# A transformer block with experts on one core: weights loaded later, products spaced wider, and the rows of expert tiles fetched ahead of their weights

## The chip, the core and the metric

The kernel runs on one core of a Trainium2 chip. A core has five engines, each with its own queue of instructions, and they run side by side. PE (TensorE) multiplies matrices and transposes, DVE (VectorE) does elementwise work, reductions and scans, ACT (ScalarE) does activation functions and copies, POOL (GpSimd) does elementwise work and indirect transfers, and SP (SyncE) does no arithmetic here: it issues transfers between HBM and the core. The metric is the device time of one execution in microseconds (us).

## The reference, cut to what matters

Four images of 256 channels and 1024 positions go through one layer: a convolutional and attention part, and then a mixture of eight experts of which two are used for each position.

```python
def _L0_conv_ref(x, ...):                       # per image; C = 256, N = 1024
    xn = layernorm(xs, norm_w, norm_b)
    xm = mamba_v(xc, ...) + skip_scale * xc     # 4 groups of channels; a scan along the 1024 positions
    Q  = conv1d(conv1d(x_concat, qdw_w, groups=NB), qpw_w)
    xgt = sigmoid(Q) * xm
    R  = conv1d(conv1d(xgt, rdw_w, groups=C), rpw_w) + xgt        # depthwise of 3 taps, then a product
    xm2 = conv1d(conv1d(concat(xs, R), fdw_w, groups=2*C), fpw_w) + xs
    x_local  = conv1d(xm2, lc_w, groups=C)
    x_global = mha(xm2, ...)                    # 8 heads over 1024 positions
    x_out = gelu(layernorm(concat(x_local, x_global) @ fc_w.T + fc_b))
    xi = conv3x3_depthwise(ln_hw(x_out)) + dwc_b
    return layernorm(xi) @ proj_w.T + proj_b

x = x + _L0_conv_ref(_ln_c(x), ...)
def _L0_ffn_ref(x, Wg, bg, W1, b1, W2, b2):     # 4096 positions, 8 experts, top 2
    top_w, top_i = top_k(x @ Wg + bg, 2);  w = softmax(top_w)
    for e in range(8):
        out += w[:, e] * (gelu(x @ W1[e] + b1[e]) @ W2[e] + b2[e])
t = t + _L0_ffn_ref(_ln_t(t), ...)
```

## The kernel before, as far as the change touches it

The kernel writes its instructions in an order of its own. Each piece of work is a Python generator; a clock of **ticks** calls each generator when it is due, and `yield k` means "go on k ticks later". The order of the calls is the order of the instructions in each engine's queue, and nothing else is decided by a tick. The backbone is the scan of the mamba part: per image 8 parts of 16 steps, one step per tick (`dBu` and `hs` on DVE, `dA` on ACT, `bs` and `yp` on PE). Everything else of the earlier image is hung between these steps.

```python
def in_turn(items, make, use, lag=2, every=1):  # products on PE (make), and what takes them away (use)
    made, lag = [], lag // every
    for at in range(len(items) + lag):
        if at >= lag:
            use(items[at - lag], made[at - lag])
        if at < len(items):
            made.append(make(items[at]))
        yield every

def depthwise3(dst, c, src, c_src, w, wi, bias):   # one tap on ACT, two on DVE, a tick between them
    nc.scalar.activation(dst[:, c, :], src[:, c_src, 0:N], AF.Identity, ...)
    yield 1
    for k in (1, 2):
        nc.vector.scalar_tensor_tensor(dst[:, c, :], src[:, c_src, k : k + N], ...)
        yield 1

def later_weights():        # weights that only later stages need, on SP's queue
    ...                     # vb, qdwT, 4 x qpwT
    for t, ap in later:     # aoutT, projT, fcT, rpwT, fpwT, wvT
        nc.sync.dma_start(t, ap)
        yield 1
    ...                     # wqkT in two transfers, qk_b in four small ones, sums on PE and DVE

def convolutions(b):
    ...                     # d[0], d[1]: depthwise results; xm: the gated image
    def residual(at, r):    # xm += product (DVE)
        ...
    yield from in_turn(CO_H, lambda at: product(f"rp_{b}...", rpwT_s, at[0], [d[1]...]), residual)
    d[1] = a8(f"d4r_{b}")
    for c in range(NC2):
        yield from depthwise3(d[1], c, xm, c, "fdw_w", NC2 + c, ...)
    def mixed(at, r):       # xl += product (DVE)
        ...
    yield from in_turn(CO_H, lambda at: product(f"fp_{b}...", fpwT_s, at[0], [d[0], d[1]...]),
                       mixed, every=1 if b == B - 1 else 2)
    yield from prepared(b)  # v, q and k of the attention

def joined(b):              # after the attention
    ...
    yield from in_turn(CO_H, lambda at: product(f"fc_{b}...", fcT_s, ...),
                       lambda at, r: nc.scalar.activation(xc[...], r, AF.Identity, ...))
    ...

def around(b): ...          # norm over the image, 3x3 taps: 18 DVE instructions into xi
def sent_off(b):            # means and variances of xi (PE), projection, routing, rows scattered (POOL)
    ...
```

After the scans of the last image PE works through 35 tiles of the experts (256 rows each), and the tail of image 3 (convolutions, attention, joining, routing; counted from 0) and the third image's `around` and `sent_off` are hung between the steps of the tiles. The tiles of the second series (8 to 15) need the third image's rows, those from 16 on the last image's.

```python
def tiles():
    def load(n):            # table of experts and rows of a new series (DVE), then 2 MB of weights (SP)
        s, i = order[n]
        if i == 0:
            tables.append(experts.series(s, temp))
        ...
        got[n] = experts.load(s, i, tables[s], w1, w2, b2_s)
    def rows(n): ...        # 256 rows of XS (260 KB), SP
    def front(n): ...       # rows transposed: xp (PE), xT (DVE)
    def ahead(n, at):       # called at each step `at` of the tile before; one thing per call
        if n < len(order) and known(n) and n not in got:
            load(n)
        elif n in got and sent(n) and n not in xs and len(got[n]) == 4:
            rows(n)
        elif n in xs and at >= 5:
            front(n)
    for n in range(len(order)):
        ...
        for at, _ in enumerate(experts.tile(n, got[n], hs, ...)):   # 8 steps: 4 x h, 4 x y
            ahead(n + 1, at)
            yield T.get(("pace",), 1)                                # ticks between two steps

PACE = {"convolutions": 1.6, "product": 2, "norm": 1.2, "taps": 0.67, "routing": 1.3, "rows": 1}
```

The weights of two tiles fit: those of tile n + 1 go where those of tile n - 1 were. PSUM has eight buffers of 128 x 512, shared by all products and by `dBu`.

Of the kernel before, what the change touches and what calls it, by code (L numbers as in the profile page):

```python
# [72 lines left out]
def network(  # L73
# [45 lines left out]
    def col(name, i=0, rows=slice(0, P)):  # L119
        at = _AT[name] + i  # L120
        return V[rows, at : at + 1]
# [22 lines left out]
    with tc.tile_pool(name="w_conv", bufs=1) as wp, tc.tile_pool(  # L144
# [53 lines left out]
        def later_weights():  # L198

            nc.sync.dma_start(vb, vbias.rearrange("a (c p) -> p (a c)", p=P))  # L200
            for t in (qdwT_s, qpwT_s, qdw_b):
                nc.gpsimd.memset(t, 0.0)
            yield 1
            nc.sync.dma_start(
                qdwT_s[:, 0 : NC2 * 3 * NB], qdwT.rearrange("p c k n -> p (c k n)")
            )
            yield 1
            for i in range(4):
                nc.sync.dma_start(qpwT_s[32 * i : 32 * i + NB, :], qpwT)
                if i % 2 == 0:  # L210
                    at = _AT["qdw_b"]
                    nc.sync.dma_start(qdw_b[32 * i : 32 * i + NB, :], vecs[0:NB, at : at + 1])
                yield 1
            for t, ap in later:
                nc.sync.dma_start(t, ap)
                yield 1
            for ci in range(NC2):
                nc.sync.dma_start(
                    wqkT_s[:, ci].rearrange("p w (i x) -> p (w i) x", x=2 * HD)
                    .rearrange("p c (i x) -> p c i x", x=HD),  # L220
                    wqkT[:, ci].rearrange("p c (i x) -> p c i x", x=2 * HD)[:, :, :, 0:HD],
                )
                yield 1
            for i in range(4):
                at = _AT["qk_b"] + i // 2
                nc.sync.dma_start(
                    qk_b[ts(i, HD), :], vecs[ds(64 * (i % 2), HD), at : at + 8 : 2]
                )
                yield 1

            obp = ps_tile("obp")
            for co in range(NC2):
                for ci in range(NC2):
                    nc.tensor.matmul(
                        obp[:, co : co + 1], aoutT_s[:, ci, ts(co, P)], vb[:, ci : ci + 1],
                        start=(ci == 0), stop=(ci == NC2 - 1),
                    )
            yield 1
            nc.vector.tensor_tensor(
                ob, obp[:, 0:NC2], V[:, _AT["attn_outb"] : _AT["attn_outb"] + NC2], ALU.add  # L240
            )

            prp = ps_tile("prp")
            for co in range(NC2):
                for ci in range(NC2):
                    nc.tensor.matmul(
                        prp[:, co : co + 1], projT_s[:, ci, ts(co, P)], col("norm_b", ci),
                        start=(ci == 0), stop=(ci == NC2 - 1),
                    )
            yield 1  # L250
            nc.vector.tensor_tensor(
                prb, prp[:, 0:NC2], V[:, _AT["proj_b"] : _AT["proj_b"] + NC2], ALU.add
            )
            for ci in range(NC2):
                nc.vector.tensor_scalar(
                    projT_s[:, ci, :], projT_s[:, ci, :], col("norm_w", ci), None, ALU.mult
                )
            yield 1

            nc.vector.tensor_reduce(fcm, fcT_s, AX.X, ALU.add)  # L260
            yield 1
            nc.vector.tensor_scalar(fcm, fcm, 1.0 / C, None, ALU.mult)
            nc.vector.tensor_tensor(
                fcT_s, fcT_s, fcm.to_broadcast([P, 2 * NC2, C]), ALU.subtract
            )
            fbp = ps_tile("fbp")
            for c in range(NC2):
                nc.tensor.matmul(
                    fbp[:, 0:1], ones_mean, col("fc_b", c), start=(c == 0), stop=(c == NC2 - 1)
                )  # L270
            yield 1
            nc.vector.tensor_tensor(
                fcb, V[:, _AT["fc_b"] : _AT["fc_b"] + NC2], fbp[:, 0:1].to_broadcast([P, NC2]),
                ALU.subtract,
            )
# [67 lines left out]
        def a8(name):  # L343
            return act8.tile([P, NC2, N], F32, tag="a8", name=name)
# [13 lines left out]
        def half(h):  # L358
            return ts(h, HALF)
# [397 lines left out]
        def convolutions(b):  # L757
# [56 lines left out]
            def residual(at, r):  # L814
# [1 line left out]
                inner = xm[:, co, ds(1 + h * HALF, HALF)]  # L816
                nc.vector.scalar_tensor_tensor(inner, r, col("rpw_b", co), inner, ALU.add, ALU.add)

            yield from in_turn(
                CO_H, lambda at: product(  # L820
                    f"rp_{b}_{at[0]}_{at[1]}", rpwT_s, at[0],
                    [d[1][:, ci, half(at[1])] for ci in range(NC2)],
                ), residual,
            )
            d[1] = a8(f"d4r_{b}")
            for c in range(NC2):
                yield from depthwise3(d[1], c, xm, c, "fdw_w", NC2 + c, col("fdw_b", NC2 + c))

            def mixed(at, r):
                co, h = at  # L830
# [4 lines left out]
                CO_H, lambda at: product(  # L835
                    f"fp_{b}_{at[0]}_{at[1]}", fpwT_s, at[0],
                    [d[ci // 2][:, ci % 2, half(at[1])] for ci in range(4)],
                ), mixed, every=1 if b == B - 1 else 2,
            )
            yield from prepared(b)  # L840

# [205 lines left out]
        def joined(b):  # L1047

            xloc, oT = XLOC.pop(b), OT.pop(b)
            pace(b, PACE["product"])  # L1050
            xglo = a8(f"xglo_{b}")
            T["attending", b] = True
            yield from in_turn(
                CO_H, lambda at: product(
                    f"ao_{b}_{at[0]}_{at[1]}", aoutT_s, at[0],
                    [oT[ci][:, half(at[1])] for ci in range(NC2)],
                ),
                lambda at, r: nc.scalar.activation(
                    xglo[:, at[0], half(at[1])], r, AF.Identity, bias=ob[:, at[0] : at[0] + 1]
                ),  # L1060
            )

            xc = XC[b] = a8(f"xc_{b}")
            both = (xloc, xglo)
            yield from in_turn(
                CO_H, lambda at: product(
                    f"fc_{b}_{at[0]}_{at[1]}", fcT_s, at[0],
                    [both[ci // 2][:, ci % 2, half(at[1])] for ci in range(4)],
                ),
                lambda at, r: nc.scalar.activation(  # L1070
                    xc[:, at[0], half(at[1])], r, AF.Identity, bias=fcb[:, at[0] : at[0] + 1]
                ),
            )

            T["joining", b] = True
            pace(b, PACE["norm"])
            yield from inverse_deviation(f"lgn_{b}", xc, b == B - 1)
            for c in range(NC2):
                nc.scalar.activation(
                    xc[:, c, :], xc[:, c, :], AF.Gelu, bias=col("lgn_b", c), scale=col("lgn_w", c)  # L1080
                )
            loaded[0] = None
            log_exp()
            yield 2
# [44 lines left out]
        def sent_off(b):  # L1129

            xc = XC.pop(b)

            def centre(h, mean):
                for c in range(NC2):
# [39 lines left out]
        def tiles():  # L1174
# [15 lines left out]
            def sent(n):  # L1190
                return T.get(("sent", B - 3 + order[n][0]))

            def load(n):
                s, i = order[n]
                if i == 0:
                    tables.append(experts.series(s, temp))
                if n == 0:
                    w1 = [a8("w1_0")[:, :, 0:DFF]]
                    w2 = [a8("w2_0").rearrange("p c (k x) -> p (c k) x", x=C)]
                else:  # L1200
                    w = [
                        acts.tile([P, N], F32, tag="dts", name=f"w_{n}_{k}") for k in range(3)
                    ] + [actd.tile([P, N], F32, tag="dt", name=f"w_{n}_3")]
                    w1, w2 = w[0:2], [v.rearrange("p (k c) -> p k c", c=C) for v in w[2:4]]
                b2_s = actc.tile([P, C], F32, tag="cs", name=f"b2_{n}") if n else a2("b2_0")[:, 0:C]
                got[n] = experts.load(s, i, tables[s], w1, w2, b2_s)
# [12 lines left out]

            def ahead(n, at):  # L1220

                if n < len(order) and known(n) and n not in got:
                    load(n)
                elif n in got and sent(n) and n not in xs and len(got[n]) == 4:
                    rows(n)
                elif n in xs and at >= 5:
                    front(n)

            for n in range(len(order)):
                while n not in got or len(got[n]) == 4:  # L1230
# [63 lines left out]
        def whole(b):  # L1294
# [2 lines left out]
        PARTS = 2 * NB  # L1297

        PACE = {
            "convolutions": 1.6, "product": 2, "norm": 1.2, "taps": 0.67, "routing": 1.3, "rows": 1  # L1300
        }
        with tc.manual_schedule(engines=ALL):
            log_exp()
# [3 lines left out]
            for b in range(B):  # L1307
                for p in range(PARTS):
                    at = b * PARTS + p
                    stop = b > 0 and p == PARTS // 2 - 1 or at == len(parts) - 1  # L1310
                    if b == 0 and p == 0:
                        start(later_weights())
                    if b == 0 and p == 2:
                        start(normalised(1))
# [729 lines left out]
```

## Time and profile before

| what | value |
|---|---|
| time, median of 3 runs | 2439.6 us (2438.16 to 2451.21) |
| span of the profiled execution | 2441.0 us, 28282 instructions |
| PE busy | 2086.5 us (85%) |
| DVE busy | 1631.0 us (67%) |
| ACT busy | 1189.7 us (49%) |
| POOL busy | 1099.7 us (45%) |
| granted PE clock, mean | 0.911 |
| DVE scan, 512 instructions | 640.0 us, 1.22 to 1.28 us each |
| first and last scan | 60.1 us, 1634.3 us |
| a tile of the experts at full rate | 14.3 us from one to the next, PE alone |

The lines of the profile are read so: line of the kernel, engine, operation, result <- operands; a wait is named by what came last. The names that matter below: `fp` and `rp` are the products of the convolutions, `fc` that of the joining projection, `xl` and `xm` what they are added into, `xi` the image under the 3x3 taps, `xs` the rows of a tile, `w` its weights, `h` and `y` its two products.

### The profile page before, as it was taken

How to read it: one execution, taken by the hardware profiler on the slowest of the kernel's cores; microseconds unless marked ns; L12 is line 12 of the kernel's file. 1: busy time of each engine (PE TensorE's matmuls, PEld its weight loads, DVE VectorE, ACT ScalarE, POOL GpSimd, SP SyncE). 2: the span in 40 equal slices, each digit the busy share in tenths (PEclk: the TensorE clock that was granted, in tenths of full speed). 3: DMA queues.
4: the chain of work that ended last, by engine and by line, in shares of the span. 5: the costliest groups of instructions: out<-in, count | busy, mean ns of one | idle time of the engine just before them, and what ended most of it. 6: DMA issues, size and time to landing. Idle time of an engine off the chain costs nothing. (4 is left out here: it accounts for less than half of the span.)

```text
span 2441.0 us, 28282 instructions
## 1 busy us (share of the span) xinstructions
PE 2086.5 (85%) x8810; PEld 933.9 (38%) x8810; DVE 1631.0 (67%) x2255; ACT 1189.7 (49%) x2013; POOL 1099.7 (45%) x1185
## 2 busy tenths in 40 slices
PE   7778767899977699987769999667999988899995
PEld 2111111332311132222113323114733667788885
DVE  3888998875899988789988877986544253211111
ACT  4553555468654458764254776325267522122221
POOL 0677777631677760466776115571130114222221
PEclk7897998999998899998689999768999999999997
DMA  3534342220234230043332102342320357566665
GB/s 88 134 109 104 83 122 70 68 60 27 73 97 109 65 84 27 22 117 83 111 87 59 47 22 66 85 156 82 92 80 1 91 154 224 171 192 199 190 197 154
DMA packets 155021, 244.32 MB, mean 100 GB/s; under 512 B 34212, under 2 KB 103492, under 8 KB 154856
## 3 DMA queue, kind: packets, MB, share of 16 engines
q1 hardware_dynamic: 135680, 217.07, 31.1%
q0 software_dynamic: 13264, 17.85, 3.7%
q10 hardware_dynamic: 5912, 7.45, 0.9%
q8 instruction: 74, 1.21, 0.2%
q14 instruction: 91, 0.75, 0.1%
HBM read 141.17 MB, written 33.98 MB: 72 GB/s over the span
## 5 line engine op out<-in xcount | busy, mean ns | idle before, releaser
L623 POOL TENSOR_TENSOR hs<-hs,cs 128x512 f32<-128x512 f32 x512 | 672.8, 1315 | 214.1 <-DVE hs L618 158.2
L604 ACT ACTIVATE dA<-dts,A 128x512 f32<-128x512 f32 x512 | 343.0, 713 | 286.1 <-DMA dts<-dt 204.5
L629 PE MATMUL yp<-hs,quads 128*32 128x512 f32 x1024 | 344.7, 687 | 151.0 <-POOL hs L623 110.5
L611 DVE TENSOR_TENSOR dBu<-dts,bs 128x512 f32<-128x512 f32 x512 | 347.7, 679 | 50.7 <-ACT xc L1070 15.3
L1911 POOL DMA_INDIRECT Y<-ys,dest x70 | 110.9, 1585 | 561.4 <-DVE ys L1905 554.9
L618 DVE TENSOR_TENSOR_SCAN hs<-dA,last,dBu 128x512 f32<-128x512 f32 x256 | 327.6, 1280 | 25.2 <-ACT low L555 0.5
L618 DVE TENSOR_TENSOR_SCAN hs<-dA,dBu 128x512 f32<-128x512 f32 x256 | 312.4, 1220 | 38.3 <-ACT dA L604 13.7
L1890 ACT ACTIVATE hs<-h,b 128x256 f32<-128x256 f32 x280 | 117.0, 472 | 385.6 <-PE h L1885 198.2
L942 ACT ACTIVATE e<-st 128x512 f32<-128x512 f32 x512 | 262.5, 607 | 74.5 <-PE st L932 71.7
L1895 PE MATMUL y<-w,hs 128*128 128x256 f32 x1120 | 261.8, 386 | 5.9 <-ACT hs L1890 5.9
L1885 PE MATMUL h<-xT,w 128*128 128x256 f32 x1120 | 252.4, 381 | 1.6 <-DVE xT L1863 1.6
L1863 DVE COPY xT<-xp 128x512 f32<-128x512 f32 x35 | 24.2, 692 | 314.0 <-PE xp L1862 299.2
L622 POOL COPY last<-hs 128x1 f32<-128x1 f32 x256 | 70.8, 277 | 355.6 <-DVE hs L618 330.6
L1895 PEld LDWEIGHTS y<-w,hs 128*128 128x128 f32 x1120 | 214.2, 194 | 41.8 <-ACT hs L1890 7.2
L596 PE MATMUL bs<-u,xpwT_s 128*32 128x512 f32 x1024 | 184.5, 698 | 52.2 <-DVE hs L618 25.8
L1885 PEld LDWEIGHTS h<-xT,w 128*128 128x128 f32 x1120 | 213.0, 191 | 38.0 <-issue 7.3
L629 PEld LDWEIGHTS yp<-hs,quads 128*32 128x32 f32 x1024 | 56.6, 119 | 412.4 <-POOL hs L623 291.1
L984 DVE TENSOR_TENSOR e<-e,e 128x512 f32<-128x512 f32 x256 | 169.8, 725 | 64.1 <-PE av L974 31.6
L932 PE MATMUL st<-qk 32*128 32x512 f32 x1024 | 190.2, 649 | 3.5 <-ACT e L942 3.0
L512 PE MATMUL up<-xn,inwk 64*128 64x512 f32 x256 | 141.5, 700 | 9.9 <-DVE hs L618 9.8
L974 PE MATMUL av<-e,v 128*32 128x512 f32 x1024 | 142.8, 620 | 0.0
L932 PEld LDWEIGHTS st<-qk 32*128 32x128 f32 x1024 | 67.9, 185 | 125.6 <-issue 86.8
(276 smaller groups left out, 2442.7 us busy)
## 6 DMA issues: line engine op xcount, KB each, us to landing
w<-in_W_dram SPq DMA_DIRECT2D x136, 512.0 KB
dts<-dt SPq DMA_DIRECT2D x512, 128.0 KB
cs<-cd SPq DMA_DIRECT2D x512, 64.0 KB
xs<-XS SPq DMA_DIRECT2D x35, 260.0 KB
b<-in_b_dram SPq DMA_DIRECT2D x35, 128.0 KB
xn<-in_x_dram SPq DMA_DIRECT2D x8, 512.0 KB
XL<-xl SPq DMA_DIRECT2D x8, 512.0 KB
xl<-XL SPq DMA_DIRECT2D x4, 1024.0 KB
```

The costliest lines, as they stand in the source:

```text
L596: nc.tensor.matmul(bs[r], xpwT_s[:, n, s : s + 1].to_broadcast([P, 32]), T[b, n, "u"][:, half(h)], start=True, stop=True,)
L604: nc.scalar.activation(dA, T[b, n, h, "dts", g][:, 0, :], AF.Exp, scale=A[:, g, n, q : q + 1])
L611: nc.vector.tensor_tensor(dBu, T[b, n, h, "dts", g][:, 1, :], T[b, n, h, "bs", q], ALU.mult)
L618: nc.vector.tensor_tensor_scan(hs, T[b, n, h, "dA", i], dBu, 0.0 if h == 0 else last, ALU.mult, ALU.add)
L623: nc.gpsimd.tensor_tensor(hs, hs, T[b, n, h, "cs", q], ALU.mult)
L629: nc.tensor.matmul(T[b, n, h, "yp"][ts(g, 32)], quads, T[b, n, h, "hs", q * GD + g], start=(q == 0), stop=(q == GS - 1),)
L932: nc.tensor.matmul(sts[i], k[r, ts(kt, P)], q[r, half(h)], start=True, stop=not shifted)
L942: nc.scalar.activation(es[i], sts[i], AF.Exp, scale=1.0 / HD**0.5)
L974: nc.tensor.matmul(accs[0][ts(i, HD)], v8[:, kt, ts(4 * g + i, HD)], es[i], start=(kt == 0), stop=(kt == NK - 1),)
L984: nc.vector.tensor_tensor(first[i], first[i], es[i], ALU.add)
L1885: nc.tensor.matmul(hp[:, i, :], w1(c, k), xT[:, c, :], start=(c == 0), stop=(c == NC2 - 1))
L1895: nc.tensor.matmul(yp[:, ts(t, C)], hs[:, k, ts(t, P)], w2(k), start=(k == 0), stop=(k == NHC - 1))
```

## The change

It moves no arithmetic and adds none: each engine has the same instructions. It changes their order.

```diff
             for t, ap in later:
                 nc.sync.dma_start(t, ap)
-                yield 1
+                yield 4                                # also after the two transfers of wqkT
 ...
-            yield from in_turn(
+            first = list(d)
+            gated = in_turn(
                 CO_H, lambda at: product(
                     f"rp_{b}_{at[0]}_{at[1]}", rpwT_s, at[0],
-                    [d[1][:, ci, half(at[1])] for ci in range(NC2)],
+                    [first[1][:, ci, half(at[1])] for ci in range(NC2)],
                 ), residual,
             )
+            for _ in range(4):
+                yield next(gated)
             d[1] = a8(f"d4r_{b}")
             for c in range(NC2):
-                yield from depthwise3(d[1], c, xm, c, "fdw_w", NC2 + c, col("fdw_b", NC2 + c))
+                for ticks in depthwise3(
+                    d[1], c, xm, c, "fdw_w", NC2 + c, col("fdw_b", NC2 + c)
+                ):
+                    next(gated, None)
+                    yield ticks
 ...                                                    # fp products of convolutions
-                ), mixed, every=1 if b == B - 1 else 2,
+                ), mixed, lag=2 if b == B - 1 else 4, every=1 if b == B - 1 else 2,
 ...                                                    # fc products of joined
-            )
+                , lag=3 if b < B - 2 else 2)
 ...
         def sent_off(b):
             xc = XC.pop(b)
+            if b == B - 2:
+                yield 6
 ...
             def ahead(n, at):
-                if n < len(order) and known(n) and n not in got:
+                if n == len(order):
+                    return
+                if n in got and len(got[n]) > 4:
+                    return
+                if n in xs and n in got and at >= 5:
+                    front(n)
+                    return
+                if known(n) and n not in tables_of:
+                    table(n)                            # the table of a series, taken out of load
+                if n not in xs and sent(n):
+                    rows(n)
+                if n not in got and known(n):
                     load(n)
-                elif n in got and sent(n) and n not in xs and len(got[n]) == 4:
-                    rows(n)
-                elif n in xs and at >= 5:
-                    front(n)
 ...
         PACE = {
-            "convolutions": 1.6, "product": 2, "norm": 1.2, "taps": 0.67, "routing": 1.3, "rows": 1
+            "convolutions": 1.4, "product": 2, "norm": 1.1, "taps": 0.67, "routing": 1.2, "rows": 1
         }
 ...
-                    if b == 0 and p == 0:
+                    if b == 0 and p == 1:
                         start(later_weights())
```

What each part is for: the late weights start one part of the scan later and stand four ticks apart, so that the scan's own transfers are not queued behind them. The residual of the second half of the channels is added while the first half is already in the next depthwise. The uses of `fp` and `fc` stand further behind their products. The third image's means are asked for six ticks later in the tail. A tile's rows are asked for before its weights. The lower paces put the steps of the tiles closer together during the convolutions, the norms and the routing of the last image.

More of the change, by code (lines that the diff above doesn't have):

```diff
@@ L222, in later_weights @@
                 )
-                yield 1
+                yield 4
             for i in range(4):
@@ L1071, in joined @@
                     xc[:, at[0], half(at[1])], r, AF.Identity, bias=fcb[:, at[0] : at[0] + 1]
-                ),
+                ), lag=3 if b < B - 2 else 2,
             )
@@ L1191, in sent, with table @@
                 return T.get(("sent", B - 3 + order[n][0]))
+            tables_of = set()
+            def table(n):
+                tables_of.add(n)
+                if order[n][1] == 0:
+                    tables.append(experts.series(order[n][0], temp))
             def load(n):
                 s, i = order[n]
-                if i == 0:
-                    tables.append(experts.series(s, temp))
                 if n == 0:
```

## The prediction

> **What bounds the kernel now.** Shares over the whole span mislead: PE is 85% busy, yet DVE sets the time for long. I read first the view of windows, with borders at the scan's parts and the tiles' starts (columns: length, busy time of PE, PEld, DVE, ACT, POOL with counts, granted PE clock, DMA share, GB/s).
>
> ```profile
> 346.00:444.00 98.00, 68.43 (x236) 16.19 (x236) 90.13 (x94) 55.19 (x77) 73.96 (x71) 0.84 0.30 81
> 444.00:655.00 211.00, 209.62 (x1034) 71.04 (x1034) 152.22 (x182) 138.66 (x247) 86.41 (x92) 0.99 0.21 56
> 655.00:749.00 94.00, 69.92 (x228) 14.62 (x226) 89.07 (x98) 51.98 (x78) 72.07 (x71) 0.94 0.39 97
> 1634.00:1672.00 38.00, 21.27 (x75) 9.57 (x74) 31.76 (x35) 17.84 (x23) 7.07 (x7) 0.72 0.56 198
> 1881.00:2133.00 252.00, 224.29 (x958) 178.06 (x958) 85.66 (x238) 80.44 (x151) 54.76 (x68) 0.95 0.51 152
> 2133.00:2404.00 271.00, 270.22 (x1289) 237.59 (x1287) 47.60 (x150) 63.82 (x152) 60.99 (x57) 1.00 0.63 181
> ```
>
> From 346 to 444 us DVE is busy 90 of 98 us and PE 68: DVE is the bound. From 444 (first `fp` product) to 655 (joining done) PE is busy 209.6 of 211: PE is the bound, and a wait of DVE in there is no loss by itself. The same pair repeats for the next two images. After 1634 PE is the bound, with holes up to 2133 and none from there to 2404.
>
> Second, what PE waited for from 1634 to 2135, and DVE from 60 to 1634 (us in total, times, longest).
>
> ```profile
> PE xp L1862 <- DMA xs<-XS: 18.5, 3, 7.7
> PE mean L387 <- DVE xi L1123: 13.9, 3, 10.5
> ```
>
> ```profile
> DVE xl L832 <- PE fp L378: 19.6, 6, 3.8
> DVE dBu L611 <- ACT xc L1070: 15.3, 4, 5.0
> DVE dBu L611 <- DMA qk_b<-in_vecs_dram: 3.2, 1, 3.2
> ```
>
> These five are what the change aims at: rows of tiles, the third image's means, spacing behind `fp`, spacing behind `fc`, late weights. Together 70.5 us. They aren't worth the same: the first two stop PE where PE is the bound, the next two stop DVE where PE is.
>
> Third, two of the holes: the timeline of PE from 1655 and that of SP from 2112 (start, length, instruction, wait before it).
>
> ```profile
> 1657.47 1.13 PE L789 MATMUL gp<-qs,qpwT_s 64*128 64x512 f32 x4
> 1660.51 1.10 PE L387 MATMUL mean<-xi,ones_mean 128*128 128x512 f32 x2 [1.92 <-DVE xi L1123]
> 1672.08 2.08 PE L387 MATMUL mean<-xi,ones_mean 128*128 128x512 f32 x2 [10.47 <-DVE xi L1123]
> 1674.09 2.08 PE L789 MATMUL gp<-qs,qpwT_s 64*128 64x512 f32 x4
> ```
>
> ```profile
> 2116.24 0.92 SPq L1842 DMA_DIRECT2D w<-in_W_dram  x2
> 2117.39 1.01 SPq L1844 DMA_DIRECT2D w<-in_W_dram  x2
> 2118.64 0.34 SPq L1845 DMA_DIRECT2D b<-in_b_dram  x1
> 2119.23 0.79 SPq L1847 DMA_DIRECT2D b<-in_vecs_dram  x1
> 2120.80 0.38 SPq L1816 DMA_DIRECT2D xs<-XS  x1
> ```
>
> A mean that isn't ready holds PE for 10.47 us, with a ready `gp` behind it. And the rows go out 4.6 us after the weights' first transfer, behind 2 MB of them; PE transposes them at 2126.9, 6.95 us late.
>
> [...] The trace: weights and rows together (2.36 MB) took 2116.24 to 2126.87. [...]
>
> **The change part by part.** The instruction orders of the two programs show the same instructions on each engine, so only waits can change.
>
> *Third image's means (six ticks, pace 1.4).* In the new order the second half of tile 0 (`y`, half of 14.3 = 7.2 us), the four transposes of tile 1 (1.1 us) and both `gp` stand ahead of the means. DVE's list before the means is the same, so they come at about the same time, and of the 12.4 us PE fills 8. A third wait of 1.5 us (image 3's mean) may close, as that mean now stands behind all of tile 8. I count 8 in all.
>
> *Rows before weights.* The three waits are 7.7 (for tile 8), 3.9 and 7.0 us (tile 16). At tiles 8 and 16 SP waits 18.1 us each for a new table, which DVE makes only once the `ys` of two tiles before are done: ready 6.7 us after tile 15 starts (2109.4 to 2116.1). That stays. New: rows out at about 7.2 us. The transposes stand at three quarters of a tile, 10.7 us. [...] the wait is gone or nearly. But the weights now go out 0.5 us later behind rows, and the next tile wants its first 1 MB at 14.4 instead of 23[...]. So each of the two events gives 5 to 5.5, the third 3.5: 14.
>
> *Lower paces.* Five tiles instead of four come before image 3's attention. That moves PE work, it removes none. Steadier PE work in 1634 to 1672 should lift the granted clock of 0.72: 2 us.
>
> *Residual inside the next depthwise.* The four `fp` products stand two ticks earlier (two scan steps). DVE skips 2 x (0.68 + 1.25) = 3.9 us of scan before PE's saturated stretch begins; PE gets those steps' work later instead: 69.9 us in 48 steps (655 to 749) is 1.46 each, 2.9. Gain 1.0, with some of PE's idle filled 1.3, three images: 4.
>
> *Spacing behind `fp`.* Uses stand at the same ticks as before, so DVE's 6.6 us per image go. But PE is saturated until 655, and the scan hangs on `bs` in PE's order: the wait moves into the attention. 0.
>
> *Spacing behind `fc`, images 0 and 1.* DVE waited 5.0, then 1.8 for `bs`, then 1.1. Without the 5.0 it meets the same `bs`, which PE delivers at 646.6 either way; the stretch ends at 655, so little of what is freed counts: 1.5 each, 3.
>
> *Late weights.* The 3.2 us wait goes; the DVE sums on the weights (5 us) stay, and transfers now stand near the second image's load: 2.
>
> Sum: 8 + 14 + 2 + 4 + 0 + 3 + 2 = 33. Less 3 for waits that new neighbours bring: 30. 2439.6 - 30 = 2410.
>
> **Rivals.** *Every wait counts.* All 70.5 less 5.0 for the last image's `fc`: 65, so 2374. For it: DVE is the bound right before and after. Against: PE 209.6 of 211.
>
> *Tiles run out.* Image 3's last routing product (`places`) now stands 3.5 tiles ahead of tile 16's transposes, 5 before: 50 us instead of 72. Scattering took from 2043 to 2089. If it takes over 50, PE waits at tile 16: 8 us or more, 2418. Against: in POOL's order the last six scatters (1.27 us apart) follow tile 13's adds and end about when tile 15 starts, ahead of the table.
>
> *Weights take the place of rows.* If the first 1 MB lands at 18 and not 15, tiles 8 and 16 start late: the gain of 14 becomes 7, 2417.
>
> *Late weights collide* with the second image's norm (DMA and SP's order): they cost 3 instead of giving 2, 2415.
>
> **Range and chances.** Down to 2388 if half of the `fp` waits count (10) and the clock gives more (10); up to 2432 if two rivals on the bad side come together (12) and new waits take 10. Faster by over 2% is below 2390.8: 0.12. Slower by over 2% needs 49 us of new waits: 0.02. The rest 0.86.
>
> **What would show it.** Right: `mean <- xi` down to about 5; `xp <- xs` under 4; in exchange up to 3 of `h` or `y` waiting for weights; `xl <- fp` near zero with PE's stretch from `fp` to joining still saturated and as long, and as much more DVE wait in the attention; end of scans 7 to 10 us earlier (1625); the tiles' end 20 to 24 earlier beyond that. Wrong: scans ending 25 us earlier (DVE's waits did count), or PE waiting for rows at tile 16 as before.

## The result, and the profile after

The changed kernel took 2405.69 us (2404.8 to 2406.01, four runs) beside 2439.8 (2438.16 to 2451.21): ratio 0.985, 95% interval 0.982 to 0.988. That is 34 us less; 30 were predicted. Measured once more beside the last experiments it took 2393.66 us (2388.99 to 2394.32), ratio 0.9811 (0.9783 to 0.9839), 46 us less; the difference between the two is taken up below.

The view of windows, with borders where the stretches begin in the changed kernel (same columns as before):

```profile
339.00:432.00 93.00, 67.78 (x220) 16.47 (x220) 84.45 (x88) 52.75 (x73) 68.45 (x64) 0.78 0.32 85
432.00:642.00 210.00, 208.35 (x1031) 70.80 (x1030) 154.81 (x186) 137.68 (x246) 89.71 (x96) 0.99 0.21 56
1620.00:1658.00 38.00, 28.61 (x114) 16.12 (x114) 32.29 (x33) 21.61 (x27) 9.64 (x8) 0.90 0.61 203
1867.00:2123.00 256.00, 247.98 (x1139) 191.78 (x1139) 96.24 (x259) 94.16 (x182) 58.88 (x71) 0.99 0.54 160
```

The regimes are the same: PE full from the first `fp` product to the end of joining (208.35 of 210 us), DVE full ahead of it. The tail's start is better filled: 28.61 of 38 us of PE at clock 0.90, where it was 21.27 at 0.72.

What PE waited for from 1634 to 2135 (us in total, times, longest):

```profile
PE mean L387 <- DVE xi L1131: 7.7, 2, 6.5
PE y L1918 <- issue: 6.1, 1, 6.1
PE st L940 <- ACT e L950: 5.1, 1, 5.1
PE pr L378 <- DVE xi L1052: 1.9, 1, 1.9
```

`xp <- xs` is gone from the list, all 18.5 us of it, and `mean <- xi` is down from 13.9. Two waits are new in this place: 6.1 us at `y` in one piece (before it was 5.9 in three, at other tiles) and 5.1 at `st` (0.9 before).

Some of what DVE waited for from 60 to 1634:

```profile
DVE hs L618 <- ACT dA L604: 21.3, 8, 4.9
DVE y L636 <- PE yp L629: 14.3, 5, 4.3
DVE dBu L611 <- ACT xc L1078: 12.2, 3, 5.0
DVE dBu L611 <- ACT u L533: 9.6, 5, 4.2
```

`xl <- fp`, 19.6 us before, is gone. Other waits rose, `hs <- dA` from 13.7, `y <- yp` from 9.7 and `dBu <- u` from 4.8: 17.0 us in all. Not all of that is the change's: `hs <- dA` reads 13.7, 8.4 and 11.9 in three kernels with the same order up to there.

The queue of SP ahead of a tile shows the new order (start, length, instruction):

```profile
2100.73 0.38 SPq L1839 DMA_DIRECT2D xs<-XS  x1
2101.67 0.93 SPq L1865 DMA_DIRECT2D w<-in_W_dram  x2
2106.81 2.11 SPq L1867 DMA_DIRECT2D w<-in_W_dram  x2
```

The rows leave 0.9 us ahead of the first weights, where they left 4.6 us after them.

**A ruler for what follows.** Three stretches of the tail repeat closely between programs: from the end of the scans to the end of tile 6, from there to the end of tile 16, and from there to the last tile. The first column is the end of the last scan, the others lie between ends of `y` products in the traces; tiles are counted from 0.

| kernel | end of scans | to tile 6 | tile 6 to 16 | tile 16 to 34 |
|---|---|---|---|---|
| before | 1634.3 | 321.7 | 191.0 | 256.1 |
| before + `fp` spacing, + late weights, + `fc` spacing (three runs) | 1627.7, 1626.3, 1639.4 | 314.7, 314.5, 315.3 | 190.6, 190.8, 190.7 | 256.1 each |
| before + rows first | 1629.6 | 315.1 | 174.5 | 256.1 |
| before + means and paces | 1638.9 | 314.3 | 195.0 | 256.1 |
| before + residual | 1638.5 | 315.3 | 197.8 | 256.1 |
| changed | 1619.8 | 316.3 | 172.5 | 256.1 |
| changed, again | 1620.3 | 305.1 | 172.5 | 256.1 |
| changed, blanks spread | 1622.8 | 305.8 | 164.1 | 256.1 |
| the same without residual | 1621.1 | 313.7 | 168.1 | 256.1 |

The end of the scans does not repeat so well: the instructions up to there are the same in "before", "rows first" and "means and paces", and it fell at 1634.3, 1629.6 and 1638.9. A few us there in one trace prove nothing; for these parts the medians count.

### The profile page after: what moved, and what is told of

The parts are those of the page before. It is cut to its first block, busy times and chain, and to the rows that moved or that the text cites. A ratio compares the mean times of both kernels' runs of the same rounds, so it can differ in the third digit from the quotient of the medians.

```text
span 2403.1 us, 28301 instructions
## 1 busy us (share of the span) xinstructions
PE 2063.8 (86%) x8810; PEld 930.1 (39%) x8810; DVE 1633.4 (68%) x2255; ACT 1186.1 (49%) x2013; POOL 1102.8 (46%) x1185
## 5 line engine op out<-in xcount | busy, mean ns | idle before, releaser
L629 PE MATMUL yp<-hs,quads 128*32 128x512 f32 x1024 | 335.3, 686 | 150.8 <-POOL hs L623 111.4
L611 DVE TENSOR_TENSOR dBu<-dts,bs 128x512 f32<-128x512 f32 x512 | 348.1, 680 | 52.2 <-ACT xc L1078 12.2
```

What stands on the lines that cost most here:

```text
L611: nc.vector.tensor_tensor(dBu, T[b, n, h, "dts", g][:, 1, :], T[b, n, h, "bs", q], ALU.mult)
L629: nc.tensor.matmul(T[b, n, h, "yp"][ts(g, 32)], quads, T[b, n, h, "hs", q * GD + g], start=(q == 0), stop=(q == GS - 1),)
```

## The experiments

Theory: the prediction's terms (rows 14, means 8, paces 2, residual 4, `fc` spacing 3, late weights 2, `fp` spacing 0). Rival: DVE's waits count in full. The first six put one part each into the kernel before; the means and the paces go together and were not separated.

**Rows ahead of weights alone.**

```diff
-                elif n in got and sent(n) and n not in xs and len(got[n]) == 4:
-                    rows(n)
+                if n not in xs and sent(n):
+                    rows(n)                  # ahead of load(n); the table taken out of load
```

> The kernel before with one part of the change alone: a tile's rows go out ahead of its weights. Theory (the hole was the rows' place in SP's queue behind 2 MB of weights, in a stretch where PE sets the time): the three waits of xp for xs, 18.5 us, go to under 4, little takes their place, time 14 to 18 us less (2422 to 2426); the end of the scans stays at 1634. Rival (the weights now come late instead): waits of h or y of about 10 us, time 7 us less.

Measured: 2416.0 us (2415.56 to 2418.11) beside 2436.51, ratio 0.9905 (0.9881 to 0.993). PE's waits, 1634 to 2135:

```profile
PE mean L387 <- DVE xi L1123: 17.2, 3, 10.5
...
PE xp L1875 <- DMA xs<-XS: 0.5, 2, 0.3
```

The wait for rows is gone. Tiles 6 to 16 take 174.5 us instead of 190.7: 16.2 us, by far the largest part of the change. One of the holes was only partly closed: with the rows there, the mean of an image holds PE for 4.82 us at 1958.5, so `mean <- xi` rises from 13.9 to 17.2. The gain, 20.5 us, is more than the 14 to 18 expected.

**Means six ticks later and lower paces alone.**

```diff
+            if b == B - 2:
+                yield 6
-            "convolutions": 1.6, ... "norm": 1.2, ... "routing": 1.3,
+            "convolutions": 1.4, ... "norm": 1.1, ... "routing": 1.2,
```

> The kernel before with only the six ticks ahead of the third image's means and the three lower paces. Theory: the wait of the means for xi falls from 13.9 to 8 us, PE has the same work, time 5 to 9 us less; the rows' waits of 18.5 us stay about as large. Rival (tiles run out ahead of the last image's rows): more wait at tile 16, time the same or longer.

Measured: 2438.38 us (2435.39 to 2443.98) beside 2436.51, ratio 1.0004 (0.9993 to 1.0015). PE's waits, 1634 to 2135:

```profile
PE xp L1864 <- DMA xs<-XS: 12.7, 2, 6.8
PE y L1897 <- ACT hs L1892: 10.1, 3, 5.1
PE mean L387 <- DVE xi L1123: 8.2, 2, 5.8
```

The means' wait shrinks as predicted, by 5.7, and the time doesn't: to tile 6 it takes 314.3 us against 314.5 to 315.3, and tiles 6 to 16 even 4.3 longer. The windows from the end of the scans to the end of tile 6 show what took the gain, first in the kernel with late weights alone, whose tail has the old order, then here:

```profile
1626.30:1940.80 314.50, 291.34 (x1413) 162.10 (x1414) 146.70 (x266) 171.36 (x294) 49.85 (x61) 0.96 0.27 79
1638.90:1953.20 314.30, 296.00 (x1414) 164.89 (x1414) 140.15 (x258) 166.07 (x290) 49.43 (x61) 0.95 0.27 80
```

PE stands idle 4.9 us less (18.3 for 23.2) and is busy 4.7 us longer with the same matmuls. The clock column is no higher over the whole stretch. With the long hole, much of the half clock falls into the hole itself and costs nothing: 9.5 of a recorded stretch of 13.65 us lie within the hole of 10.47. With the hole shortened, more of it falls on work, 24.4 us in this stretch where it was 16.3.

After tile 6 a new hole of 5.11 us at `y` (2081.7) is part of the loss. ACT's timeline ahead of that hole:

```profile
2075.62 10.58 ACTq L1482 DMA_DIRECT2D XS<-blank  x8
2086.25 3.02 ACT L1892 ACTIVATE hs<-h,b 128x256 f32<-128x256 f32 x8 [17.96 <-DMA XS<-blank]
```

Eight transfers that the last image's routing issues on ACT hold it for 10.58 us, and all eight gelus of a tile stand behind them.

**Residual inside the depthwise alone.**

```diff
+            gated = in_turn(... residual)
+            for _ in range(4):
+                yield next(gated)
 ...
-                yield from depthwise3(d[1], c, xm, c, ...)
+                for ticks in depthwise3(d[1], c, xm, c, ...):
+                    next(gated, None)
+                    yield ticks
```

> The kernel before with only the residual drawn into the next depthwise (its products of fp follow two ticks earlier, their uses two ticks earlier too). Theory (what counts is that the fp products, the start of PE's saturated stretch, stand two ticks earlier): fp starts about 4 to 6 us earlier after the start of its image, the stretch is 2 to 3 us longer, so 2 to 3 us per image and 6 to 9 us in all, with the wait of xl for fp still there. Rival (the spacing behind fp is what helped): less than 2 us.

Measured: 2446.75 us (2434.29 to 2451.3) beside 2436.51, ratio 1.0028 (1.0014 to 1.0042): slower. PE's waits, 1634 to 2135:

```profile
PE places L1605 <- DVE oh L1598: 4.1, 1, 4.1
```

In the kernel before `places` waited 1.7 us, for `ex`. The wait lies in the last image's routing, between tiles 6 and 16, which take 197.8 us instead of 190.7, so 7.1 of the 10 us are there. In the first three images `fp` starts 5.7, 3.8 and 7.2 us earlier after the start of its image, about as expected, but the stretch from `fp` to joining grows to 211.9, 213.3 and 213.7 us from 206.9, 209.3 and 207.8. Of the earlier start 1.8 us are left over three images.

**Spacing behind `fp` alone.**

```diff
-                ), mixed, every=1 if b == B - 1 else 2,
+                ), mixed, lag=2 if b == B - 1 else 4, every=1 if b == B - 1 else 2,
```

> The kernel before with only the wider spacing behind the fp products. Theory (PE is saturated there, a wait of DVE is worth nothing): the wait of xl for fp falls from 19.6 us to under 3, waits of DVE for ACT and for PE rise in its place in the same parts of the scan, the stretch from fp to the end of the joining keeps its 207 to 209 us, time within 2 us of before. It also delays v, q and k by two ticks, which may cost up to 3 us. Rival (every wait of DVE counts): 15 to 20 us less.

Measured: 2431.73 us (2424.51 to 2444.12) beside 2436.51, ratio 0.998 (0.9965 to 0.9994). `xl <- fp` is gone, but `y <- yp` rises from 9.7 to 18.2 and `dBu <- u` from 4.8 to 13.4: 17.1 of the 19.6 us come back under other names. The stretches from `fp` to joining are 205.3, 206.5 and 204.7 us long, 1.5 to 3.2 shorter than before. As `fp` starts a little later, the better measure goes from the start of an image to the end of joining: 307.6 to 305.7 in the second and 313.8 to 310.8 in the third, where the three kernels with the old order agree to 0.2. So a third or so of the 6.6 us of DVE wait per image counts, though PE is full there.

**Late weights alone.**

```diff
-                yield 1
+                yield 4                       # at both places
 ...
-                    if b == 0 and p == 0:
+                    if b == 0 and p == 1:
                         start(later_weights())
```

> The kernel before with only the late weights (one part of the scan later, four ticks apart). Theory (fewer transfers between the scan's own in its second part; the sums on the weights move from the second part to the fourth): second part 33 us instead of 41, fourth 44 instead of 39, first image 277 to 281 us from first scan to the second image's, where five runs of the early order took 280 to 290; time 3 to 6 us less. Rival (they collide with the second image's norm): first image no shorter, time the same or 3 us more.

Measured: 2435.37 us (2426.62 to 2439.72) beside 2439.41, ratio 0.9983 (0.9973 to 0.9994). The eight parts of the first image's scan tell where. The second takes 33.0 us in all six traces with late weights and 40.6 to 42.1 in all eight others; the fourth takes 44.4 in those six, and 39.1 (once 40.3) in the others. So 8 us leave the second part and 5.3 come back in the fourth, where the sums on the weights now stand. The 3 us that remain are about the size of the wait for a transfer (`qk_b` or `cs`) in the second part: 2.7 to 3.9 us in seven of the eight, and none in the six.

**Spacing behind `fc` alone.**

```diff
-            )
+                , lag=3 if b < B - 2 else 2)
```

> The kernel before with only the wider spacing behind the fc products of images 0 and 1. Theory (PE delivers bs when it does; only what DVE gets ahead by the end of the joining counts): the wait of dBu for ACT's xc falls by about 1 us per image, that for bs rises by the same, time 0 to 3 us less. Rival (the 5.0 and 4.1 us waits of DVE count): 7 to 9 us less.

Measured: 2432.66 us (2429.54 to 2442.97) beside 2439.41, ratio 0.9973 (0.9957 to 0.9988). DVE's `dBu <- xc` falls from 15.3 to 12.2 us in this trace. That accounts for 3; the median gained 6.8, and I can't place the rest.

**Residual and `fp` spacing together.** The two edits above in one kernel.

> The kernel before with the residual drawn into the depthwise and the wider spacing behind fp, together. Theory now, after the two alone (residual alone: fp starts 4 to 7 us earlier, but the stretch to the joining's end grows by 4 to 6 us): the products earlier and their uses in the old place is what pays, so fp starts 4 to 6 us earlier, the stretch grows by only 2 to 3, about 9 us over three images; time 6 to 10 us less. Rival (the parts merely add): the stretch grows by 4 or more again and the time is within 3 us of before.

Measured: 2436.78 us (2429.3 to 2447.08) beside 2439.41, ratio 0.9994 (0.9982 to 1.0007). In the first three images the theory holds: against the kernel before `fp` starts 6.1, 4.0 and 5.6 us earlier and the stretch grows by only 2.9, 1.3 and 1.8. But tiles 6 to 16 take 197.4 us, 6.4 more, nearly as with the residual alone: the spacing doesn't take that loss away.

**The changed kernel with its eight blank-row transfers spread.** The new hole at `y` in the changed kernel is explained by ACT's timeline and PE's:

```profile
2045.05 10.50 ACTq L1503 DMA_DIRECT2D XS<-blank  x8
2055.65 3.02 ACT L1913 ACTIVATE hs<-h,b 128x256 f32<-128x256 f32 x8 [18.73 <-DMA XS<-blank]
```

```profile
2056.17 5.67 PE L1918 MATMUL y<-w,hs 128*128 128x256 f32 x16 [6.11 <-issue]
```

The same burst of blank rows, 10.50 us, stands ahead of all eight gelus of tile 13. The list of waits says only "issue"; ACT's queue shows the cause. The experiment issues one after each of the first eight scatters.

```diff
-            self.blank_ends()                 # eight transfers at once, on ACT
+            ends = self.blank_ends()          # now returns a function that issues one of them
 ...
                 self.sent.append(ins)         # after each scatter
+                if b == self.B - 1 and j * NT + t < NE:
+                    ends(j * NT + t)
```

> The changed kernel with one more edit: the eight transfers of blank rows on ACT's queue, one after another before the last image's rows are scattered, are issued one at a time between the scatters instead. Theory (in the changed kernel these transfers hold ACT for 10.5 us, and PE waits 6.1 us for the gelu of tile 13): that hole goes, the stretch from the last scan to the last tile falls from 744.8 to about 739, time about 5 us less than the changed kernel (about 2400). Rival (the scattered rows now wait for ACT, and tile 16 waits for them): a wait of xp for xs appears at tile 16 and the time is no less.

Measured: 2384.73 us (2382.48 to 2389.15) beside 2439.41, ratio 0.9765 (0.9741 to 0.9788). This version beats both kernels. ACT's timeline:

```profile
2039.91 0.38 ACTq L1503 DMA_DIRECT2D XS<-blank  x1
2040.33 0.84 ACT L1917 ACTIVATE hs<-h,b 128x256 f32<-128x256 f32 x2 [0.46 <-issue]
2041.13 0.38 ACTq L1503 DMA_DIRECT2D XS<-blank  x1
2041.56 0.84 ACT L1917 ACTIVATE hs<-h,b 128x256 f32<-128x256 f32 x2 [0.38 <-issue]
```

The gelus pass between the transfers, and the hole is gone. But the gain on the first measurement is 21 us, from a hole of 6.1; the next two runs ask why.

**The changed kernel again.** No edit; a second profile.

> The changed kernel once more, for a second profile. If its 5.1 us hole in image 3's attention (PE at st, waiting for e) belongs to the program, it is there again, and the time is 2404 to 2407; then it explains 8.5 of the 21 us between this kernel and the one with spread blanks. If it was a matter of one execution, it is gone and the tail is 736 us long, though the median stays at 2404 to 2407, and those 8.5 stay unexplained.

Measured: 2393.66 us, given above. The stretch to tile 6 is 305.1 us, where it was 316.3: the hole at `st` is gone, and nothing else of the tail changed. In the first trace ACT stood still there:

```profile
1800.70 0.60 ACT L950 ACTIVATE e<-st 128x512 f32<-128x512 f32 x1 [0.35 <-PE st L940]
1807.86 2.06 ACT L950 ACTIVATE e<-st 128x512 f32<-128x512 f32 x4 [6.57 <-remote]
```

That is 6.57 us with no work and no releaser that the trace records ("remote"). Against the second trace PE falls behind by 10.8 us within a few dozen matmuls there and keeps that distance to the end. The trace of the kernel before has the like at the same instructions of image 3's attention, where it costs 5.8 us (its 321.7 against 314.5 to 315.3 contains it); no trace of the experiments has it. What stopped ACT stays open. Both traces of the pair first measured have it, so it is no effect of the change. Nor does it explain the whole step from 34 to 46 us: within the pair it cost the changed kernel only 5.0 us more, and the kernel before took as long in the last measurement (2439.53) as in the first (2439.8). The expectation that the median would stay at 2404 to 2407 was wrong; whether all four executions of the first measurement had the stop is not shown, as one was traced. Compared with the second measurement, spreading the blanks brings 8.9 us, and 8.4 between tiles 6 and 16 (172.5 to 164.1), for a hole of 5.37 in that trace.

**Five holes made on purpose.** Why does a hole cost more than its length? In the trace of the kernel before, 13.65 us of half clock begin within the 10.47 us wait for `xi`, and 6.83 within the 6.95 us wait for rows. In the kernel with spread blanks, ACT repeats the seventh gelu of five tiles.

```diff
-            for i in range(2):
+            again = {18: 8, 21: 12, 24: 16, 27: 24, 30: 32}.get(j, 0) if k2 == 3 else 0
+            for i in [0] * again + [0, 1]:
                 k = 2 * k2 + i
                 nc.scalar.activation(hs[:, k, :], hp[:, i, :], AF.Gelu, ...)
```

> The changed kernel with spread blanks (2384.7 us), and on ACT, ahead of the last two hs of tiles 18, 21, 24, 27 and 30, 8, 12, 16, 24 and 32 more gelus of 0.42 us each into the same place, so that PE, full there, must wait before y's seventh product: holes of about 2.7, 4.3, 6.0, 9.4 and 12.7 us, 35 in all. Theory (a hole is paid for again in the granted clock: after each one PE runs at half clock for about the hole's length, in steps of 3.4 us, which costs half of that): half-clock stretches of 3.4, 3.4, 6.8, 10.2 and 13.7 us, 19 more, 2384.7 + 54 = 2438. Rival (a hole costs its length): 2384.7 + 35 = 2420, no half clock between 1750 and the last tile.

Measured: 2433.87 us (2430.58 to 2441.05), 49.1 more than without holes. PE's timeline over the third of them, and the windows before the holes and right after this one:

```profile
2214.07 2.07 PE L1923 MATMUL y<-w,hs 128*128 128x256 f32 x4 [6.08 <-ACT hs L1918]
2215.94 1.06 PE L1889 MATMUL xp<-ident,xs 128*128 128x128 f32 x4
2216.80 4.27 PE L1923 MATMUL y<-w,hs 128*128 128x256 f32 x16
```

```profile
2092.00:2106.00 14.00, 14.00 (x68) 12.32 (x68) 2.54 (x8) 3.36 (x8) 3.14 (x3) 1.00 0.67 190
2214.00:2218.00 4.00, 3.93 (x11) 3.24 (x12) 0.93 (x3) 0.39 (x2) 0.00 (x0) 0.50 0.00 0
```

In the 4 us after the hole the clock column is 0.50, and `y` products start 0.43 us apart instead of 0.22. Tile by tile, against 14.25 us for a tile without a hole:

| hole (us) | tile longer by (us) | beyond the hole | half clock recorded (us) |
|---|---|---|---|
| 2.03 | 3.98 | 1.95 | 3.4 |
| 4.05 | 6.00 | 1.95 | 3.4 |
| 6.08 | 8.32 | 2.24 | 6.8 |
| 10.14 | 12.12 | 1.98 | 10.2 |
| 14.19 | 17.41 | 3.22 | 17.1 |

So the theory is right in kind and wrong in size. A hole is paid for again, but by about 2 us up to 10 us of hole and by 3.2 at 14, not by half its length. The two short stretches of half clock lie wholly behind their holes; the three long ones begin within them, where PE has nothing to slow down, and only 4.0, 3.5 and 6.0 us lie behind. The sum, 47.8, is nearly the difference of the runs. The kernel before shows the same: its tile 15, with the 6.95 us wait for rows, takes 23.2 us, 2.0 more than a full tile and the wait. In the traces of the kernel before and of the changed one every record of the granted clock is 1.00 or 0.50, and all but the last of each trace are 3.41 us long or a multiple of it (110 and 94 records); the five stretches of the table fit that. The shortest hole, of 2.03 us, already cost 1.95 more.

**Spread blanks and rows first, with the old paces and means.** The first experiment's kernel with the spread blanks.

> The kernel before with rows ahead of weights (2416.0 us) and the eight blank-row transfers spread over the scatters; means and paces as before. Theory (the burst of blanks on ACT holds up a tile's hs only where the lower paces and the later means have put tile 13's gelus beside it; with the old paces no such hole is in the trace): 2413 to 2418. Rival (the burst costs in any order: 6.1 of hole and 3.4 of half clock): 2406.

Measured: 2418.66 us (2412.5 to 2424.48) beside 2439.53, ratio 0.9911 (0.9881 to 0.9941). That is at the theory's end of the forecasts (2413 to 2418), not at the rival's. Tiles 6 to 16 take 174.4 us, 174.5 without the spread. With the old means and paces the burst does no harm: in the kernel with rows first alone it runs from 2040.76 for 9.60 us, but behind a tile's gelus instead of ahead of them. With the means and paces moved alone it stood ahead of eight. So the `y` hole belongs to that part of the change.

**Spread blanks without the residual's move.**

```diff
-            gated = in_turn(...)              # and the loop with next(gated, None)
+            yield from in_turn(... residual)  # as in the kernel before
```

> The changed kernel with spread blanks, and with the residual of the convolutions where the kernel before has it, outside the depthwise. Theory (the residual's new place costs, as it did alone, +10 us, and with the fp spacing, +5): 2384.7 less 5 to 10, so 2375 to 2380, the first three images shorter by 2 each. Rival (it gains beside the other parts, as predicted, 4): 2389. Second rival (other waits close the difference): 2384 to 2386.

Measured: 2399.36 us (2393.43 to 2405.88) beside 2439.53, ratio 0.984 (0.9805 to 0.9874): 15 us slower than with the residual's move. My theory, that the residual's move makes the whole slower, falls. The scans end at about the same time (1621.1 and 1622.8), but a small cost in the first three images isn't excluded: without the move a longer stretch of half clock made the third part of the first image take 43.4 us instead of 39.1, and the move doesn't reach that part. The tail is 11.9 us longer without it, 7.9 of it before tile 6. ACT's timeline there, first without the residual's move:

```profile
1920.21 1.57 ACT L1909 ACTIVATE hs<-h,b 128x256 f32<-128x256 f32 x4
1921.65 2.38 ACT L1079 ACTIVATE xc<-xc,V 128x1024 f32<-128x1024 f32 x2
1924.05 1.28 ACT L365 ACT_TABLE_LOAD   x1
1925.34 1.28 ACT L1909 ACT_TABLE_LOAD   x1
1926.63 0.84 ACT L1909 ACTIVATE hs<-h,b 128x256 f32<-128x256 f32 x2
```

and then with it:

```profile
1921.37 2.30 ACT L1917 ACTIVATE hs<-h,b 128x256 f32<-128x256 f32 x6
1923.52 2.40 ACT L1087 ACTIVATE xc<-xc,V 128x1024 f32<-128x1024 f32 x2
```

Without it the last image's own two gelus (`xc`) and two table loads of 1.28 us stand between the gelus of tile 6, and PE waits 4.43 us at `y`. With it they stand behind six of the gelus and the wait is 0.57. That 4.43 us hole is in the kernel before, and in those with rows, means and paces, or residual alone. The residual's move puts ACT's block behind the gelus only beside the other parts; which of them it needs was not separated.

## Why the prediction held, step by step

**Rows, 14: right, a little small.** 16.2 us on the ruler, 20.5 and 20.9 in two medians. The mechanism held (table wait stays, rows out at once, transposes no longer waiting), and the feared exchange did not come: no `h` or `y` waits for weights. How soon rows and weights land, and with it the 5 to 5.5 us per event, was an estimate; in the changed kernel's trace the rows of tiles 8 and 16 leave at 1943.82 and 2086.92 us, and PE transposes them 2.7 and 3.3 us later. Nor did the tiles run out: the wait at tile 16 is gone. The tiles show where the sum erred: tile 12, with the 3.91 us wait and 0.94 at `y`, gets 7.0 us shorter and tile 15, with the 6.95, 8.5, so these two brought 2.2 and 1.5 us beyond their waits, which the sum lacked. Tile 7, with the 7.68, gets only 3.0 shorter, since the mean behind it now waits 4.82 us where it waited 1.53; tiles 10 and 11 lose 1.7 together. What the medians show beyond the ruler is not placed.

**Means 8, and "steadier PE work ... should lift the granted clock", 2: the step that failed.** Alone they gave nothing (ratio 1.0004), though the wait shrank by 5.7. The granted clock of the first 38 us behind the scans does rise, to 0.85 with them alone. But of the 21 us of half clock behind the old 0.72, 9 lay within the 10.47 us hole and cost nothing; with the hole shortened more half clock fell on work, and PE needed 4.7 us more for the same matmuls, about what it stood idle less. With the residual's move and the other parts beside them, the stretch to tile 6 falls from 315.1 to 305.1, so the 10 us are there, but for another reason in good part: the `y` hole of 4.43 us closes too, and PE's busy time stays at 291.5. The changed kernel then gives 8.4 back at tile 13.

**Residual, 4: wrong in place, and alone in sign.** In the first three images the `fp` products do come earlier, by 4.1, 6.9 and 4.5 us (from the start of the image, with and without the move in the kernels with spread blanks), but the stretch after them is longer by 4.2, 7.6 and 5.7. The prediction let part of PE's idle time be filled; up to the end of joining that pair shows 2.0 us lost over three images, the move alone 1.8 gained, and the move beside the `fp` spacing 5.3 gained. A gain of 4 there is neither shown nor excluded. Its large effect is in the last image's tail: 7.1 us lost alone, 11.9 gained beside the other parts.

**`fp` spacing, 0: too low.** Ratio 0.998, about 5 us. DVE's waits under a full PE weren't worth nothing, yet the rival "every wait counts" (19.6 us) is off too.

**`fc` spacing 3, late weights 2: of the right size.** Medians say 6.8 and 4.0; the traces account for 3 in each.

**Waits that new neighbours bring, 3: too low.** The burst of blanks alone costs 8.4.

**The test points.** The tail was to end 20 to 24 us earlier beyond the scans: 24.0 in the first pair of traces, 27.9 when traces without ACT's stop are compared (314.8 + 190.7, the means of the three spacing and weight runs, against 305.1 + 172.5). The scans were to end 7 to 10 us earlier: 14.5 and 14.0, where programs with equal orders up to there differ by 9. `mean <- xi` went to 7.7 instead of 5. The sum of 30 lay close to 34 and further from 46, because the terms too small (what the clock takes after a hole, `fp`, `fc`, the interplay of residual and paces) outweighed those that failed. That the total came so near is in part luck: terms of 14 us in all (means 8, clock 2, residual 4) gave nothing or a loss when tried alone, and the range's lower end, 2388, should by its own two tens have been 2390.

## What to carry to other kernels

Where an engine is full, price a hole at its length plus what the clock takes afterwards (1.95 to 3.22 us for the five holes here), and move a small transfer that it will wait for ahead of the large ones in its queue (16.2 us less between tiles 6 and 16 here). A clock that reads low over a stretch with a hole in it is no gain waiting to be fetched: look at whether the half clock falls on work (behind the 0.72 here, 9 of 21 us fell into the hole). Parts of a reordering don't add: the same residual move cost 7 us alone and brought 12 beside the others, so test a part by taking it out of the whole as well as by putting it in alone. After each gain look at the new list of waits; here it named a burst on a helper engine whose spreading brought 9 us more.

## What the runs showed of the hardware

- Five holes of 2.03 to 14.19 us in a full PE, in one trace, cost 1.95 to 3.22 us each beyond their length, with 3.4 to 17.1 us of half clock recorded at each.
- Half-clock stretches also move between programs with the same instructions. In the first image's third part the longest such stretch was 6.8 us in nine traces and 13.7 to 30.7 in the five others; DVE's wait for `bs` was 2.5 to 3.1 us in the nine and 7.2 in the five, and the part took 38.6 to 39.2 and 43.4 to 47.6 us. This is one source of the 9 us by which the scans' end varies.
- Eight transfers to addresses from registers took ACT 10.50 us in a row in the changed kernel, and 0.38 us for each of the three that went between gelus alone in the kernel with spread blanks.
- ACT stood still for 6.57 us with no recorded cause in the changed kernel's first trace, and PE fell 10.8 us behind there.
